# Diagonal tiles for the channels' own term, and a later store of the first batch's inputs, in a three-part decoder layer

## The chip, the core and the metric

One core of a Trainium2 chip runs the whole layer in one launch. The core has a matrix engine (TensorE, "PE" in the profile; its weight loads are "PEld"), a vector engine (VectorE, "DVE"), an activation engine (ScalarE, "ACT"), a general engine (GpSimd, "POOL") and a queue engine that mostly issues DMAs (SyncE, "SP"). ACT issues DMAs too. Each engine executes its own instructions strictly in the order in which they were laid down when the program was built, so an instruction that waits holds everything behind it on that engine, DMA issues included.

The metric is device time in microseconds (us) of one execution; lower is better.

## The reference, cut to what matters

Inputs are `x` (4 batches of 512 tokens by 512 channels), a context `ctx_1024` (4 by 512 by 256) and weights, all float32. Three sublayers follow one another, each with a residual sum and a layer norm:

1. Windowed attention: compress 512 channels to 256, make q, k and v, softmax attention with 16 heads in windows of 128 tokens with a relative bias, project back to 512.
2. A selective state-space layer (SSM). It takes the context as its input and the normed attention output as its gate `z`.
3. A gated feed-forward with quantized activations and ternary weights (512 to 2048 and back).

The change touches the second one. Its core, cut:

```
u     = silu(conv(in_proj_w @ ctx) + conv_b)          # 512 channels x 512 steps, per batch
x_dbl = x_proj_w @ u                                  # dt_lo (16 rows), Bm (16), Cm (16)
delta = softplus(dt_proj_w @ dt_lo + dt_proj_b)
state = state * exp(delta * A) + (delta * u) * Bm     # along time, 512 channels x 16 states
y     = sum over the 16 states of state * Cm
y     = y + D * u                                     # the channels' own part
out   = y * silu(z)
```

The last sum, `D * u`, is what the change calls the channels' own part of the outputs.

## The kernel before, in words

**Staging.** Every batch goes through three kinds of work: attention (threads `attn_c`, `attn_qk`, `attn_window`), the SSM (`ssm_inputs`, `ssm_steps`, `ssm_gate`) and the feed-forward (`ffn`, with `ffn_signs` turning the weights into signs once, by way of memory). Each of these is a Python generator. A weaver takes them in turn by times written out by hand (the constants `TP`, `T0`, `TA`, `TG`, `DT` and so on) and gives the instructions priorities from that. A planner then settles the order on each engine when the program is built, from these priorities, from data dependences, from free buffers and from its own model of how long each instruction takes. There is no run-time reordering between engines: what the planner laid down is what every queue does. So an edit at one place can alter the order elsewhere.

**The SSM's inputs (`ssm_inputs`).** Per batch, the projection and the convolution write `u`, a tile of 128 partitions by 4 channel groups (`e` = 0 to 3) by 512 steps. The whole `u` is stored to memory as `ud` (line 290, issued by ACT, 1 MB). Then PE makes `xd` from `u` (line 296), ACT copies it (line 297), and its B and C rows are stored as `bcd` (line 299, issued by ACT, 64 KB). `ssm_weights` loads these rows back, spread over partitions, as `bc` (line 347, issued by SP). PE makes `dt` (line 307), ACT the softplus into `sizes`. Line 319 then multiplies `sizes` by `u` **in place**, one instruction for each `e`: on DVE for the first batch, on POOL for the others. For the first batch's first channel group the product and `sizes` are spread over partitions by PE (line 328, tiles `du_ps` and `d_ps`) and copied out by DVE (line 332) and ACT (line 330). All other groups are stored as `dd` and `dud` (lines 335 and 336, SP) and loaded back spread out (line 367, SP).

**The SSM's steps (`ssm_steps`).** A batch has four channel groups `q` of 128 channels. A partition holds one of 32 channels with one of 4 states, so a group takes 4 channel blocks `j` (in two pairs `g`) times 4 state sets `n`. Per pair and `n`: POOL multiplies `du` by B (line 384), ACT makes `da` (line 388), DVE runs the recurrence (line 390), and DVE (line 392) or POOL (line 394) multiplies by C. PE then sums the 4 states of each channel into the output `y`, a PSUM bank of 128 channels by 512 steps. Block `j` goes to the 32 partitions from 32j on, as a matmul of 128 rows by 32 columns placed in column tile j (line 398, a float32 matmul is two instructions on PE). There is one `y` bank (`BY = 1`).

The group's own part opens that sum. `uq`, the group's slice of `ud`, is loaded by SP (line 355), and line 374 multiplies it by `own`, a 128 by 128 diagonal matrix of `D`:

```
with tc.issue_after(ssm_dt[0].ins) if b + q == 0 else ExitStack():
    nc.tensor.matmul(y, lhsT=own[:, q, :], rhs=uq, start=True, stop=False)
```

This happens 16 times (4 batches by 4 groups), 32 instructions on PE. For the first group of the first batch it is held behind the last spread matmul of line 328.

**Buffers.** The tag `yr` has two buffers of 128 by 512 (`BR = 2`). Before the change only `ssm_gate` uses them, to load finished outputs `y` back (line 425).

**DMA completion.** The issues of the SP and ACT queues take turns on eight completion counters, and an issue waits until the earlier transfer on its counter has landed.

## Time and profile before

| what | value |
|---|---|
| runs of before | 831.76, 842.35 and 834.16 us, median 834.16 us |
| the profiled execution | 833.79 us, its span on the core 832.0 us |
| mean granted TensorE clock | 0.951 of full speed |
| PE busy by stretch: 0 to 100 us | 82.9 of 100 us |
| PE busy, 100 to 500 us | 379.5 of 400 us |
| PE busy, 500 to 700 us | 170.0 of 200 us |
| PE busy, 700 us to the end | 121.6 of 132 us |
| first and last product of the SSM's steps (POOL, line 384) start at | 38.86 and 672.81 us |

How to read it: times in the profile are microseconds from the start of the span. A row of the timeline is start, duration, engine, line, operation, output<-inputs, shapes and count, and in square brackets how long the engine was idle before it and what ended the idle time. "SPq" and "ACTq" rows are DMA issues on those queues. "xN" is how many instructions a row merges; instructions on PE are pipelined and can overlap, so the time of a PE group is best taken from its start to the start of the next row. The chain of waits names, from the last instruction backwards, what released each step.

### The profile page before, as it was taken

The page shows a single profiled execution, that of the slowest core. Times are in us where ns is not written, and L with a number is a line of the kernel's source. Part 1 is how long each engine was busy: PE and PEld are TensorE (multiplying, and loading weights), DVE is VectorE, ACT ScalarE, POOL GpSimd, SP SyncE. Part 2 cuts the span into 40 slices and gives each one's busy share as a digit, 9 for nine tenths or more (in the row PEclk, how much of TensorE's full clock was granted, in tenths as well). Part 3 has the DMA queues.
Part 4 walks back from the last instruction along what each step waited for, and adds up shares of the span by engine and source line. Part 5 has one row for each costly group of instructions (what it writes and reads, how often), then busy time and mean ns, then how long its engine had stood idle before and what let it go on. Part 6 is the DMA issues. An engine that isn't in the chain of part 4 may idle for free.

```text
span 832.0 us, 11692 instructions
## 1 busy us (share of the span) xinstructions
PE 754.0 (91%) x3906; PEld 411.9 (50%) x3906; DVE 647.7 (78%) x943; ACT 591.2 (71%) x1037; POOL 557.4 (67%) x323
## 2 busy tenths in 40 slices
PE   9798899999899999899988998798887889999995
PEld 4233244444344444344434454365455657777773
DVE  5279586898999887989989799989999588453542
ACT  3568789787775976877797868696685847845651
POOL 2177489598678779787865968787889383333342
PEclk9797899999899999999999999999899999999998
DMA  7887688876243438564334384772251202301101
GB/s 216 300 275 222 225 263 306 307 220 211 91 140 103 149 83 264 190 230 143 107 108 126 106 288 170 216 275 97 94 162 37 70 8 102 95 20 51 52 26 51
DMA packets 82497, 128.97 MB, mean 155 GB/s; under 512 B 18659, under 2 KB 29043, under 8 KB 81157
## 3 DMA queue, kind: packets, MB, share of 16 engines
q1 hardware_dynamic: 65700, 108.51, 40.2%
q10 hardware_dynamic: 16736, 19.71, 6.9%
q8 instruction: 31, 0.51, 0.3%
q14 instruction: 30, 0.24, 0.1%
HBM read 91.22 MB, written 36.97 MB: 154 GB/s over the span
## 4 chain that ended last, share of the span: by engine, by line
PE 53%; DVE 20%; ACT 14%; DMA 5%; issue 5%; POOL 2%; SPq 1%; ACTq 0%; DVEq 0%; POOLq 0%
PE d_ps L824 9%; DVE da L390 6%; PE y L398 5%; PE sc_ps L628 5%; PE u_ps L796 4%; DVE state L390 4%; PE g_ps L772 3%; PE a_ps L695 3%; PE sc_ps L619 3%; ACT da L388 3%; PE c_ps L562 2%; PE sc_ps L656 2%; DVE state L392 2%; PE in_ps L273 2%; PE xd_ps L296 2%
## 5 line engine op out<-in xcount | busy, mean ns | idle before, releaser
L384 POOL TENSOR_TENSOR state<-du,bc 128x1024 f32<-128x1024 f32 x128 | 301.7, 2373 | 112.7 <-PE y L398 65.7
L388 ACT ACTIVATE da<-d,a_neg 128x512 f32<-128x512 f32 x256 | 174.9, 695 | 71.0 <-DVE state L392 37.7
L394 POOL TENSOR_TENSOR state<-state,bc 128x1024 f32<-128x1024 f32 x64 | 152.1, 2377 | 41.4 <-DVE state L390 27.5
L390 DVE TENSOR_TENSOR_SCAN state<-da,state 128x512 f32<-128x512 f32 x128 | 152.8, 1210 | 30.0 <-ACT da L388 21.6
L390 DVE TENSOR_TENSOR_SCAN da<-da,state 128x512 f32<-128x512 f32 x128 | 153.2, 1215 | 11.1 <-ACT da L388 11.1
L817 POOL TENSOR_TENSOR lo<-gs,hi 128x512 fp32r<-128x512 f32 x64 | 81.9, 1286 | 105.5 <-ACT hi L815 102.3
L398 PE MATMUL y<-state,sel 128*32 128x512 f32 x512 | 98.5, 649 | 6.4 <-DVE state L392 3.6
L392 DVE TENSOR_TENSOR state<-da,bc 128x512 f32<-128x512 f32 x128 | 84.9, 679 | 0.7
L652 ACT ACTIVATE sc<-sc_ps,ntop 128x128 f32<-128x128 f32 x256 | 74.0, 375 | 12.0 <-DVE ntop L636 10.9
L824 PE MATMUL d_ps<-sd,hi 128*128 128x512 f32 x256 | 74.5, 412 | 8.3 <-DVE gs L780 4.3
L772 PE MATMUL g_ps<-taken,sg 128*128 128x256 bf16 x512 | 69.4, 280 | 9.0 <-DVE x L867 4.3
L824 PE MATMUL d_ps<-sd,lo 128*128 128x512 f32 x256 | 75.7, 418 | 0.0
L628 PE MATMUL sc_ps<-k,q 32*128 32x256 f32 x256 | 73.6, 410 | 1.0 <-ACT q L584 1.0
L815 ACT CAST hi<-gs 128x512 fp32r<-128x512 f32 x64 | 38.8, 614 | 50.0 <-DVE gs L805 33.2
L796 PE MATMUL u_ps<-taken,su 128*128 128x256 bf16 x512 | 67.5, 273 | 6.7 <-DVE gs L805 5.5
L805 DVE TENSOR_TENSOR gs<-gs,u_ps 128x512 f32<-128x512 f32 x64 | 43.5, 682 | 38.3 <-PE u_ps L796 38.0
L780 DVE TENSOR_TENSOR gs<-g_ps,taken 128x512 f32<-128x512 f32 x64 | 43.4, 682 | 30.5 <-PE g_ps L772 30.5
L772 PEld LDWEIGHTS <-sg 128*128 128x128 fp8e4 x512 | 47.7, 100 | 33.7 <-issue 28.1
L796 PEld LDWEIGHTS <-su 128*128 128x128 fp8e4 x512 | 46.3, 98 | 29.0 <-issue 21.2
L628 PEld LDWEIGHTS sc_ps<-k,q 32*128 32x128 f32 x256 | 42.5, 187 | 30.1 <-issue 23.5
L824 PEld LDWEIGHTS d_ps<-sd,hi 128*128 128x128 f32 x256 | 45.0, 191 | 22.7 <-ACT hi L815 4.2
L636 DVE TENSOR_REDUCE ntop<-sc_ps 128x4 f32<-128x512 f32 x64 | 43.3, 679 | 15.1 <-PE sc_ps L628 15.0
(161 smaller groups left out, 1184.0 us busy)
## 6 DMA issues: line engine op xcount, KB each, us to landing
d<-dd SPq DMA_DIRECT2D x60, 256.0 KB, 4.3
du<-dud SPq DMA_DIRECT2D x60, 256.0 KB, 4.1
bc<-bcd SPq DMA_DIRECT2D x32, 256.0 KB, 4.3
xT<-in_xT_dram SPq DMA_DIRECT2D x16, 256.0 KB, 4.8
xa<-in_x_dram SPq DMA_DIRECT2D x16, 256.0 KB, 4.6
raw_sgd<-in_wgT_dram SPq DMA_DIRECT2D x16, 256.0 KB, 3.7
ud<-u ACTq DMA_DIRECT2D x4, 1024.0 KB, 8.2
uq<-ud SPq DMA_DIRECT2D x16, 256.0 KB, 2.7
```

The costliest lines, as they stand in the source:

```text
L384: nc.gpsimd.tensor_tensor(st, du, bb.unsqueeze(1).to_broadcast([P, 2, S]), ALU.mult)
L388: nc.scalar.activation(da, d[:, j, :], AF.Exp, scale=a_neg[:, a : a + 1])
L390: nc.vector.tensor_tensor_scan(to, da, st[:, j, :], 0.0, ALU.mult, ALU.add)
L392: nc.vector.tensor_tensor(st[:, j, :], da, cb, ALU.mult)
L394: nc.gpsimd.tensor_tensor(st, st, cb.unsqueeze(1).to_broadcast([P, 2, S]), ALU.mult)
L398: nc.tensor.matmul(y[ts(j, EB), :], lhsT=sel, rhs=sts[j], start=False, stop=(n == NG - 1), tile_position=(0, EB * j))
L628: nc.tensor.matmul(psc[:, ts(m, 2 * P)], lhsT=qT[rows_, m, tok], rhs=kT[rows_, m, :, tok], start=False, stop=(m == NM - 1), tile_position= ...
L652: nc.scalar.activation(sc[:, j, :], psc[:, ts(j, P)], AF.Exp, bias=ntop[:, h : h + 1])
L772: nc.tensor.matmul(pg[:, ts(j, HS)], lhsT=sg[:, c, ts(2 * f2 + j, P)], rhs=qT[:, c, :], start=(c == 0), stop=(c == NC - 1),)
L796: nc.tensor.matmul(pu[:, ts(j, HS)], lhsT=su[:, c, ts(2 * f2 + j, P)], rhs=qT[:, c, :], start=(c == 0), stop=(c == NC - 1),)
L817: nc.gpsimd.tensor_tensor(lo, g2, hi.bitcast(F32), ALU.subtract)
L824: nc.tensor.matmul(pos[t], lhsT=part[:, j, ts(t, P)], rhs=sd[:, 2 * f2 + j, :], start=(f2 + j == 0 and part is parts[0]), stop=(f2 == NF2 ...
```

## The change

Three edits, all in the SSM.

1. The own part is no longer one 128 by 128 matmul per group but four of 32 rows by 32 columns, the blocks on the diagonal of the same `own` tile, block `j` reading partitions 32j on of `uq`, writing partitions 32j on of `y`, and placed at row and column 32j of the array. Each opens its part of the sum.
2. For the first batch only, the store of `u` to `ud` is issued after the store of `bcd` and not before the `xd` matmuls.
3. For the first batch only, the products of `sizes` and `u` go to tiles of their own, named `due`, in the two buffers of tag `yr`, and not over `u`. The four products take these two buffers in turn.

```
-        nc.scalar.dma_start(out=ud, in_=u)
+        if b > 0:
+            nc.scalar.dma_start(out=ud, in_=u)
...
         nc.scalar.dma_start(out=bcd, in_=xd[DB:XD, :])
+        if b == 0:
+            nc.scalar.dma_start(out=ud, in_=u)
...
-            adder.tensor_tensor(u[:, e, :], ex, u[:, e, :], ALU.mult)
+
+            due = mp.tile([P, S], F32, tag="yr", name=f"due{e}", bufs=BR) if b == 0 else u[:, e, :]
+            adder.tensor_tensor(due, ex, u[:, e, :], ALU.mult)
...
-                    for k, src in (("du", u[:, e, :]), ("d", ex)):
+                    for k, src in (("du", due), ("d", ex)):
...
-            nc.sync.dma_start(out=dud[:, e, :], in_=u[:, e, :])
+            nc.sync.dma_start(out=dud[:, e, :], in_=due)
...
-                nc.tensor.matmul(y, lhsT=own[:, q, :], rhs=uq, start=True, stop=False)
+                for j in range(NQ):
+                    part = ts(j, EB)
+                    nc.tensor.matmul(
+                        y[part, :],
+                        lhsT=own[part, q, part],
+                        rhs=uq[part, :],
+                        start=True,
+                        stop=False,
+                        tile_position=(EB * j, EB * j),
+                    )
```

`NQ` is 4, `EB` is 32, and `ts(j, n)` is the slice from j times n to (j + 1) times n.

## The prediction

> **What bounds the kernel now.** I read the page's busy line first, then the chain of waits, then the order of time around the first product of the SSM, then PE's rows around line 374.

> ```profile
> PE 754.0 (91%) x3906; PEld 411.9 (50%) x3906; DVE 647.7 (78%) x943; ACT 591.2 (71%) x1037; POOL 557.4 (67%) x323
> ```

> No engine is full, but PE is near it: 379.5 of the 400 us from 100 to 500. The SSM's steps form the long thread, from 38.86 us to about 690; the list of waits shows POOL's products idle 65.7 us, in 27 stands, for line 398 to release state buffers, so PE's order sets that thread's pace. The feed-forward follows. Two things can therefore move the end: when the thread starts, and PE's time in it.

> The chain of waits at the start (start, length, what):

> ```profile
> 20.43 4.68 DMA xT<-in_xT_dram
> 25.18 8.23 DMA ud<-u
> 33.52 0.70 DVE u L319
> 34.27 3.78 PE du_ps L328 x4
> ```

> The store of `u` is on the path because line 319 overwrites `u`: it must wait until the store has read it. The same in order of time:

> ```profile
> 25.18 0.38 ACTq L290 DMA_DIRECT2D ud<-u  x1
> 25.61 0.68 ACT L297 ACTIVATE xd<-xd_ps,col 49x512 f32<-49x512 f32 x1 [2.99 <-DMA xT<-in_xT_dram]
> ...
> 26.96 0.35 ACTq L299 DMA_DIRECT2D bcd<-xd  x1
> ...
> 28.63 2.10 ACT L309 ACTIVATE sizes<-dt_ps 128x512 f32<-128x512 f32 x4
> ...
> 33.43 0.33 SPq L355 DMA_DIRECT2D uq<-ud  x1
> 33.52 2.50 DVE L319 TENSOR_TENSOR u<-sizes,u 128x512 f32<-128x512 f32 x4 [12.64 <-DMA ud<-u]
> 33.86 1.29 SPq L347 DMA_DIRECT2D bc<-bcd  x2
> ...
> 38.86 2.35 POOL L384 TENSOR_TENSOR state<-du,bc 128x1024 f32<-128x1024 f32 x1 [32.61 <-DVE du L332]
> ```

> Two stands end with the same landing. DVE was ready when the first softplus was (one takes 0.60 us, so 28.63 + 0.60 = 29.23) and starts at 33.52. SP issues nothing between 24.9 and 33.43, because its next instruction, `uq`, reads `ud`; the first `bc` loads stand behind it.

> **The products elsewhere: −4.2 us.** The in-place hazard goes. What is late next is the softplus, so line 319 starts near 29.28 instead of 33.52: 4.24 us. From there to the first POOL product took 5.34 us (one product, four `du_ps` passes, the copy), giving 34.6 instead of 38.86. If PE, with no idle time ahead of it, does its four passes in 1.9 us (row 40.68 us: 1.88 for four) and not 3.78, it is up to 1.9 us more.

> The tag `yr` has two buffers. The third product waits until the last `du_ps` pass has read the first `due` (its end was about 42.4, now about 38.2), and the fourth until the second one's `dud` store has landed (3.4 us median). Behind them on DVE stand copies of line 332 and the first scans. I cost this at nothing: DVE idles 2.96 us ahead of the copy at 41.74 and 3.15 ahead of the scan at 48.69, and the third group's first `dud` load is issued at 74 us, the fourth's later. Without that cover it is one landing, 3.4 us.

> **The store behind the projections: 0, bounds −0.7 and +1.7 us.** Both issues stay on ACT, in the other order; nothing is added. ACT issued `ud` at 25.18 after waiting for an earlier transfer's counter, and `bcd` at 26.96 for the next counter. Swapped, line 297 can begin when `xd_ps` ends (about 24.95) instead of 25.61, 0.66 us sooner, `bcd` goes at about 25.7, and `ud` at about 26.95 on the later counter, so the table load ahead of the softplus stays at 27.3. `bcd` (64 KB; stores of that size, the `sgd` ones, land in 3.5 us) is there by 29.2, `bc` (4.7 us) by 34.0: just ahead of the 34.6 above, if SP lets it go. The `ud` store now ends near 26.95 + 8.23 = 35.2, 1.8 us later, and `uq` with it. The first own pair ran at 45.83 and its first partner on line 398 at 53.65, so even moved 4 us forward it has `uq` (35.2 + 0.3 + 2.7 = 38.2) ahead of 41.5. If `uq` still stands ahead of `bc` or of the `dd` stores on SP, that queue stands until 35.2: +1.7.

> **The diagonal tiles: +1.5 us.** PE's rows, whose costs are from one start to the next:

> ```profile
> 100.05 1.07 PE L398 MATMUL y<-state,sel 128*32 128x512 f32 x8
> 101.04 0.50 PE L619 MATMUL sc_ps<-bias_hi,identr 128*128 128x512 f32 x1
> ...
> 131.32 1.02 PE L374 MATMUL y<-uq,own 128*128 128x512 f32 x2
> 132.27 0.43 PE L663 MATMUL a_ps<-scT,v 128*32 128x128 f32 x8
> ...
> 251.29 1.06 PE L398 MATMUL y<-state,sel 128*32 128x512 f32 x6
> 252.28 0.66 PE L656 MATMUL sc_ps<-ident,sc 128*128 128x128 f32 x4
> 252.87 1.04 PE L398 MATMUL y<-state,sel 128*32 128x512 f32 x2
> 253.85 0.33 PE L656 MATMUL sc_ps<-ident,sc 128*128 128x128 f32 x1
> ```

> Four column tiles take 0.99 us, three 0.99, one alone 0.98: tiles in different columns run side by side, and their number costs nothing. The own pair took 0.95 (two passes of 0.43 plus 0.09 where the array's shape changes). Eight diagonal instructions side by side take the 0.99 of the row x8. What is added is a change of shape on the side where there was none: at most 0.09 us for each of 16, 1.5 us in all. There is no gain in PE time to be had from this edit alone.

> No row shows tiles on different rows *and* columns. The bounds: one after another, eight passes of 0.43 are 3.43 us, 2.57 more than the 0.86 of now, 16 times, +41 us of PE. Below nothing: if they slip entirely under neighbouring tiles, 16 × 0.95 = −15 us. The nearest row, line 398, is the same bank, the same columns and the same form, so I take it. A second price: the planner may lay other matmuls between the four. Of line 398's 64 sums, 38 stand whole and the rest in pieces of 0.98 each; 0.44 extra pieces per sum would be 16 × 0.44 × 0.98 = 6.9 us. But those pieces come of states that are ready at different times, while the four own tiles wait for one load; I keep 6.9 for the range alone.

> [...]

> **The sum.** Against the profiled execution (832.0 us of span, 833.79 in all, 0.4 below the median of 834.16): 833.8 − 4.2 + 0 + 1.5 = 831.1, so **831 us**. The 4.2 should carry: the thread that starts earlier runs through stretches where PE always has work.

> **The rivals.**

> *The SP stand was the real brake: about 813 us.* For: SP sends everything late after 33.43, the first sign stores too; ACT then stands 3.91 us at 46.24 and 1.24 at 51.76 for sign stores, and 1.76 at 57.20, with the states' `da` behind it. If SP starts 4.9 us sooner (28.5) and these 6.9 us go too, that is 11.8; if the new order also spares the longest stand of POOL for line 398 (9.3 us), 21. Against: the DMA engines are busy 84% from 20 to 40 and 91% from 40 to 60, so earlier issues mostly queue.

> *The stand only moves: about 837 us.* `uq` stays ahead on SP, now until 35.2 (+1.7); the first `bc` lands after 39 and eats the 4.2; the fourth product's wait costs another part of its 3.4. 833.8 + 1.7 + 1.5 = 837. This is also the case in which the change doesn't do what it says.

> *The tiles do not run side by side: about 859 us, slower.* 11 of the 16 own pairs lie between 98 and 465 us, where PE is 95% full; 11 × 2.57 = 28 us, 831 + 28 = 859 (all sixteen: 872). It decides the sign at 2% once an own group costs over (850.8 − 831)/16 = 1.2 us more than now. An order in which PE makes the states wait for a split own group ends at the same place.

> **Chances.** Forecast 0.37, moved stand 0.15 (both within 2%, which is about what a measurement of this kernel can tell from no change: its runs span 831.76 to 842.35); SP as brake 0.26; tiles in a row or split on the path 0.22. The edits change the planner's order from 25 us on, and I cannot read that order from here; I hold the two outer cases this high because POOL's 65.7 us of stands for PE show how much lies in it. The forecast's own range, with −1.9 and +6.9 as its ends, is 829 to 838. For 8 times in 10 the range takes half of each outer case: 812 to 857. Faster by over 2% 0.25, within 0.53, slower 0.22.

> **What would show it.** Right: line 319 on DVE starts near 29.3 with no wait for `ud`; the first POOL product near 34.6; `bc` issued before `uq`; own instructions of 32 by 32 in groups of eight, about 1.0 us to the next row. Wrong: SP idle to 35; own instructions 0.43 us apart or in pieces; or the starts as predicted and the last line 398 no earlier than 687, in which case the order lost what the start gained.

## The result and the profile after

The changed kernel takes **874.25 us** (median; 871.40 to 878.20), the kernel before beside it 838.25 us (831.76 to 843.78). The ratio is **1.0451 [1.0394, 1.0508]**: slower by 4.5%, where 831 us was forecast and 857 was the upper end of the range. The profiled execution has a span of 876.4 us (878.20 in all), so 44.4 us are to be found against the 832.0 of before. (The medians lie 36 us apart: the profiled execution of after is the slowest of its four, and that of before, 833.79 us, is faster than the median.) Ratios here and below leave out executions that ran in a slower state, among them one of `b_diag` that took 1057.84 us at a mean clock of 0.637, while the medians in us are of all executions.

The page of the kernel after, with its first part and the granted clock of TensorE from its second (tenths of full speed in 40 slices; a 9 is 90% or more):

```profile
span 876.4 us, 11890 instructions
...
PE 795.4 (91%) x4002; PEld 424.1 (48%) x4002; DVE 654.9 (75%) x943; ACT 590.3 (67%) x1037; POOL 558.1 (64%) x323
...
PEclk9798969589989989898769998979999999999998
```

The same clock line of before:

```profile
PEclk9797899999899999999999999999899999999998
```

PE is busy for 41.4 us more with only 96 more instructions; the sums of DVE, ACT and POOL have moved by about 1% or less. The mean granted clock fell from 0.951 to 0.909. In the trace the clock is only ever full or half, and it was half for 160.9 us instead of 83.7. (Such times are taken here to the end of the execution, some 1.8 us behind the span's.)

**Where the 44.4 us lie.** The last product of the SSM's thread (line 384 before, 398 after) starts at 696.65 us instead of 672.81, which is 23.8 us. Behind it follow 179.8 us instead of 159.2, the other 20.6. These are two different losses.

*Ahead of the last product* the clock is at half for 153.6 us instead of 75.1. These 78.5 us more could cost up to 39 (an estimate: half of them), which is enough for the 23.8; whether they do is tested below. The same stretch by the windows view (stretch, length, busy us and count of PE, PEld, DVE, ACT and POOL, mean granted clock, DMA share, GB/s), of before:

```profile
100.00:200.00 100.00, 97.51 (x481) 45.20 (x480) 80.79 (x100) 82.92 (x172) 82.26 (x38) 0.95 0.81 271
```

and of after:

```profile
100.00:200.00 100.00, 94.09 (x386) 40.32 (x385) 69.92 (x83) 72.67 (x147) 66.95 (x31) 0.80 0.66 223
```

PE is busy nearly as long, but at a clock of 0.80 it gets through 386 matmuls instead of 481, and POOL through 31 instructions instead of 38. In the list of waits POOL's stands (times in which an engine stands idle and waits) for PE to release state buffers grow from 65.7 us to 81.8.

*Behind the last product* the clock is full in both kernels (0.98 and 0.99); there is more work left. PE is busy for 166.68 us from 697 to 876, and for 146.08 us from 673 to 832 before. PE's groups in those stretches (instructions, busy us, mean ns, idle before), of before:

```profile
L824 PE MATMUL d_ps<-sd,lo 128*128 128x512 f32 x164 | 47.1, 409 | 0.0
L824 PE MATMUL d_ps<-sd,hi 128*128 128x512 f32 x160 | 46.9, 413 | 1.5 <-ACT hi L815 0.9 <-DVE gs L780 0.6
L796 PE MATMUL u_ps<-taken,su 128*128 128x256 bf16 x312 | 41.1, 274 | 0.3 <-DVE gs L780 0.3
L772 PE MATMUL g_ps<-taken,sg 128*128 128x256 bf16 x256 | 33.4, 273 | 1.7 <-DVE gs L780 0.9 <-DVE x L867 0.7
```

and of after:

```profile
L838 PE MATMUL d_ps<-sd,lo 128*128 128x512 f32 x186 | 53.9, 409 | 0.0
L838 PE MATMUL d_ps<-sd,hi 128*128 128x512 f32 x184 | 53.6, 410 | 0.4 <-ACT hi L829 0.3
L810 PE MATMUL u_ps<-taken,su 128*128 128x256 bf16 x360 | 47.7, 274 | 0.7 <-DVE gs L819 0.7
L786 PE MATMUL g_ps<-taken,sg 128*128 128x256 bf16 x296 | 38.8, 273 | 1.7 <-DVE gs L794 0.9 <-DVE gs L819 0.8
```

Each matmul costs what it did, but 134 more of them (22 + 24 + 48 + 40) have been left for the end: work that before's order laid under the SSM.

**The start.** In order of time:

```profile
25.68 0.38 ACTq L302 DMA_DIRECT2D ud<-u  x1
...
26.82 0.35 ACTq L300 DMA_DIRECT2D bcd<-xd  x1
...
29.12 0.69 DVE L324 TENSOR_TENSOR due<-sizes,u 128x512 f32<-128x512 f32 x1 [7.62 <-ACT sizes L312]
...
33.07 0.33 SPq L360 DMA_DIRECT2D uq<-ud  x1
...
33.49 1.28 SPq L352 DMA_DIRECT2D bc<-bcd  x2
...
39.76 0.69 DVE L324 TENSOR_TENSOR due<-sizes,u 128x512 f32<-128x512 f32 x1 [8.59 <-ACT da L402]
40.38 0.68 DVE L337 COPY du<-du_ps 128x512 f32<-128x512 f32 x1
...
42.04 0.67 DVE L337 COPY du<-du_ps 128x512 f32<-128x512 f32 x1
...
42.80 2.34 POOL L398 TENSOR_TENSOR state<-du,bc 128x1024 f32<-128x1024 f32 x1 [36.37 <-DMA bc<-bcd]
```

The first product runs at 29.12, as forecast (29.3), but then DVE stands for 8.59 us ahead of the third one, with the copies of line 337 behind it. POOL begins at 42.80 instead of 38.86; its bracket names `bc`, but the second copy, which ends at 42.71, is what came just ahead of it. The store `ud` still goes ahead of `bcd`, and `uq` still ahead of `bc`.

**The tiles.** PE's rows around an own part that stayed whole, and around one that did not:

```profile
131.29 1.06 PE L381 MATMUL y<-uq,own 32*32 32x512 f32 x8
132.28 0.50 PE L707 MATMUL a_ps<-rows,one 2*128 2x512 f32 x1
...
409.78 1.74 PE L381 MATMUL y<-uq,own 32*32 32x512 f32 x2
411.45 3.78 PE L273 MATMUL in_ps<-hT,in_s 128*128 128x512 f32 x4
415.17 1.92 PE L381 MATMUL y<-uq,own 32*32 32x512 f32 x4
...
420.17 1.91 PE L381 MATMUL y<-uq,own 32*32 32x512 f32 x2
```

Eight instructions of four tiles take 0.99 us to the next row: they run side by side. At 409.78 the planner has laid other matmuls between the tiles of one group; the three pieces take 1.67 + 1.84 + 1.84 = 5.35 us at half clock.

So my reading was: neither the tiles' form nor the start is worth 44 us, and what is new is the order on every engine. The theories to be told apart were: **order** (the planner's new order makes the loss, whatever the tiles do), **form** (32 by 32 tiles cost PE time or clock), and **start** (the 4 us at the start grow on the way).

### The profile page after: what moved, and what is told of

It is laid out like the page before. It is cut to its first block, busy times and chain, and to the rows that moved or that the text cites. A ratio compares the mean times of both kernels' runs of the same rounds, so it can differ in the third digit from the quotient of the medians.

```text
span 876.4 us, 11890 instructions
## 1 busy us (share of the span) xinstructions
PE 795.4 (91%) x4002; PEld 424.1 (48%) x4002; DVE 654.9 (75%) x943; ACT 590.3 (67%) x1037; POOL 558.1 (64%) x323
## 3 DMA queue, kind: packets, MB, share of 16 engines
q1 hardware_dynamic: 65700, 108.51, 38.2%
## 4 chain that ended last, share of the span: by engine, by line
PE 43%; DVE 22%; ACT 10%; issue 7%; DMA 4%; POOL 3%; SPq 0%; ACTq 0%; DVEq 0%; POOLq 0%
PE d_ps L838 11%; DVE da L404 6%; DVE state L404 5%; PE y L412 5%; PE u_ps L810 5%; PE g_ps L786 4%; PE sc_ps L642 4%; PE sc_ps L633 2%; DVE state L406 2%; PE sc_ps L670 2%; ACT da L402 2%; PE y L381 2%; DMA acc<-x0d 2%; POOL state L398 2%; PE dt_ps L310 1%
## 5 line engine op out<-in xcount | busy, mean ns | idle before, releaser
L398 POOL TENSOR_TENSOR state<-du,bc 128x1024 f32<-128x1024 f32 x128 | 302.2, 2376 | 145.8 <-PE y L412 81.8
L402 ACT ACTIVATE da<-d,a_neg 128x512 f32<-128x512 f32 x256 | 177.0, 700 | 74.6 <-DVE state L406 40.2
L412 PE MATMUL y<-state,sel 128*32 128x512 f32 x512 | 101.3, 666 | 10.1 <-DVE state L406 9.7
L642 PE MATMUL sc_ps<-k,q 32*128 32x256 f32 x256 | 80.3, 438 | 0.0
L642 PEld LDWEIGHTS sc_ps<-k,q 32*128 32x128 f32 x256 | 46.3, 202 | 31.4 <-issue 25.2
L670 PE MATMUL sc_ps<-ident,sc 128*128 128x128 f32 x256 | 48.0, 321 | 9.3 <-ACT sc L666 9.1
```

The source lines that it names most:

```text
L398: nc.gpsimd.tensor_tensor(st, du, bb.unsqueeze(1).to_broadcast([P, 2, S]), ALU.mult)
L402: nc.scalar.activation(da, d[:, j, :], AF.Exp, scale=a_neg[:, a : a + 1])
L412: nc.tensor.matmul(y[ts(j, EB), :], lhsT=sel, rhs=sts[j], start=False, stop=(n == NG - 1), tile_position=(0, EB * j))
L642: nc.tensor.matmul(psc[:, ts(m, 2 * P)], lhsT=qT[rows_, m, tok], rhs=kT[rows_, m, :, tok], start=False, stop=(m == NM - 1), tile_position= ...
```

## The experiments

### Form and order, each without the other

`b_diag` takes before's order as it was laid down and replaces the own part's instructions where they stand; the first new one inherits the old one's waits, the last its releases. `a_full` does the opposite in the order of after.

```diff
+def swap_own(nc):                      # once the order is laid down; b_diag, on before
...
+        new = [
+            nc.tensor.matmul(
+                y[ts(j, EB), :],
+                lhsT=own[ts(j, EB), q, ts(j, EB)],
+                rhs=uq[ts(j, EB), :],
+                start=True,
+                stop=False,
+                tile_position=(EB * j, EB * j),
+            )
+            for j in range(NQ)
+        ]
...
+        # a_full, on after:
+        new = [nc.tensor.matmul(y[:, :], lhsT=own[:, q, :], rhs=uq[:, :], start=True, stop=False)]
```

> Every engine keeps the order of the kernel before, instruction for instruction; alone the 16 own pairs are replaced where they stand by the four diagonal tiles each (no other edit). Theory O (the planner's new order costs the time): no slower than before by over 1%, 834 to 842 us, since 16 changes of shape are worth 1.5 us. Theory T (the diagonal tiles themselves cost it, by running one after another or by letting the matrix engine's clock drop): 855 us or more, with more of the span at half clock than the 84 us of before.

> Every engine keeps the order of the changed kernel; alone the own parts are put back to one 128 by 128 matmul each, where the first of the four tiles stood. The products' own tiles and the later store stay. Theory O: as slow as the changed kernel, 866 to 878 us. Theory T: back to 834 to 845 us. If both have a share, it is read from the two runs together: this one less before is the order with the other two edits, the changed kernel less this one is the form of the tiles.

| order | own part whole | own part as four tiles |
|---|---|---|
| before's | 1 | b_diag: 834.74 us, 0.9969 [0.9935, 1.0004] |
| after's | a_full: 864.74 us, 1.0342 [1.0293, 1.0391] | after: 874.25 us, 1.0451 [1.0394, 1.0508] |

The four tiles cost nothing that can be told in before's order. After's order with the whole matmul back in it is 3.4% slower (it still has the other two edits, see below). So most of the loss is the order's. The form adds about 1% within it by these two rows, but that share is not firm: `own_alone` below has nearly the same order and the split tiles without the other two edits, and cannot be told from `a_full`.

The trace of `b_diag` shown here comes from one more execution of the same program:

> The same program as the run with before's order and diagonal tiles, looked at once more for a profile at the usual clock (the first one was taken in an execution of 1057.84 us at a mean clock of 0.637). Theory O: 16 groups of eight own instructions, each about 0.99 us to the next row at full clock, time at half clock near before's 84 us, span 828 to 842 us. Theory T: over 110 us at half clock.

It took 832.54 us beside 832.49 for before; its span is 830.8 us, the clock 0.953, the last product starts at 671.6 us, with 159.1 us behind it. The own part's instructions, by its tile view (ns least/median/most, first and last start):

```profile
L946 PE MATMUL y<-uq,own x128: 587/600/612, 45.3 to 662.9; 32*32 32x512 f32 x128
```

Of the 16 groups, 14 take 0.991 us to the next row. **Form is out, for an order in which the four stand together.**

### One edit at a time, each with its own order

`own_alone` has the first edit only (four matmuls in place of one, and the planner lays down what it will); `due_alone` only the products in buffers of their own.

> Only the diagonal tiles, planned as a whole; products in place, store as before. The order it is given is the changed kernel's to over 99% on PE, DVE and SP and wholly on ACT and POOL. Theory O and theory T: 866 to 878 us, as the changed kernel. A value in the middle would say that the start's stall (the products) had a large share after all.

> Only the products' own tiles; the own part is one matmul and the store of u stands where it stood. The order on ACT and POOL is that of before, PE, DVE and SP keep 99% of theirs. In the changed kernel DVE stood 8.6 us ahead of the third product, which was laid ahead of the copies of the spread products, so the first POOL product started at 42.8 us and not at 38.9. Theory: this alone does the same, first product at 42 to 43 us, and the span grows by at most those 4 us: 834 to 842 us. The prediction's step (first product at 34.6 us) would give 830.

`own_alone`: 868.86 us, 1.0369 [1.0300, 1.0439]. Its last product starts at 691.0 us with 179.8 us behind it: the whole loss, nearly, from this edit. Its order parts from before's after PE's first 42 matmuls. By the longest sequence that two orders have in common, 83% of PE's instructions stand as in before's order, 62% of DVE's and 65% of ACT's (the expectations below count more narrowly and give lower shares). Against after, 99% is the same.

`due_alone`: 840.98 us, 1.0017 [0.9967, 1.0068]. Its order is before's, but for 1%. At the start, its DVE rows:

```profile
29.43 1.29 DVE L321 TENSOR_TENSOR due<-sizes,u 128x512 f32<-128x512 f32 x2 [9.17 <-ACT sizes L309]
39.97 0.69 DVE L321 TENSOR_TENSOR due<-sizes,u 128x512 f32<-128x512 f32 x1 [9.24 <-DMA dud<-due]
40.58 0.68 DVE L334 COPY du<-du_ps 128x512 f32<-128x512 f32 x1
```

Two products run early; the third takes a buffer of `yr` whose content is still being stored to `dud`, and waits 9.24 us for that landing (in after, where the bracket of the same stand names an ACT instruction that ended at that moment, it is 8.59). The first POOL product comes at 43.01, 4.15 us later than before, and the end is not measurably later.

The second edit alone, the store moved behind the projections, was not run: with it the planner lays down the same order on every engine as without it.

### Is any new order that bad?

If before's order is one good draw among many, an edit that adds next to no work must cost too, as soon as it makes the planner lay down something else. Four kernels change one of the hand-written constants by a little; three add no instruction, and `null_warm` adds one warming matmul at the start, some 0.9 us:

```diff
-TP = (-45, 50, 100, 170)
+TP = (-45, 51, 100, 170)     # null_tp
-AQ = 18
+AQ = 17                      # null_aq
-WARM = 3
+WARM = 4                     # null_warm
-AW = 10
+AW = 10.2                    # null_aw
```

> The kernel before with one hand-written time moved by one unit (the second batch's inputs due at 51, not 50). No instruction is added or taken away; the planner then gives PE 63%, DVE 45%, ACT 43% of the old order. Theory O1 (the order before is a chosen one, and nearly any other costs some per cent): 848 to 875 us. Theory O2 (something in the four tiles makes the changed kernel's order bad, other orders do not): 830 to 846 us. In both the span should stand at 790 to 800 us plus half of the time that the matrix engine's clock is at half, as in the five traces so far.

> The kernel before with the start of the attention's q and k moved by one unit (17 ahead of a batch's first window, not 18). No work added; PE keeps 62%, DVE 36%, ACT 34% of the order. O1: 848 to 875 us. O2: 830 to 846 us.

> The kernel before with a fourth warming matmul at the start (one pair more on PE at 5 us, 0.9 us). PE keeps 84%, DVE 54%, ACT 36% of the order. O1: 848 to 875 us. O2: 830 to 846 us.

> The kernel before with the distance between attention windows at 10.2 units, not 10. No work added; PE keeps 79%, DVE 60%, ACT 54% of the order, the nearest of the four to before. O1: 840 to 875 us. O2: 830 to 846 us.

| kernel | us, ratio [95%] | PE's order kept | half clock, us | last product starts | behind it |
|---|---|---|---|---|---|
| before | 836.78 beside the next four, 838.75 beside `own_alone` | | 83.7 | 672.8 | 159.2 |
| null_tp | 903.23, 1.0769 [1.0694, 1.0844] | 80% | 165.3 | 758.5 | 144.7 |
| null_aq | 861.33, 1.0279 [1.0215, 1.0344] | 81% | 93.9 | 680.6 | 176.4 |
| null_warm | 859.17, 1.0253 [1.0195, 1.0312] | 84% | 114.3 | 703.4 | 156.3 |
| null_aw | 849.23, 1.0169 [1.0080, 1.0258] | 85% | 90.4 | 678.7 | 164.0 |
| own_alone | 868.86, 1.0369 [1.0300, 1.0439] | 83% | 150.7 | 691.0 | 179.8 |

All four are slower, by 1.7 to 7.7%, and `null_tp` lies above the 848 to 875 us that were expected for it. The loss lies now ahead of the last product, now behind it, now in both. Nor does the clock explain all of it. The expectation's sum was 790 to 800 us plus half of the time at half clock; the span less that half is 798 us for `null_aw`, but 803 for `null_warm`, 810 for `null_aq` and 820 for `null_tp`, whose last product comes 85.7 us later with only 81.6 us more at half clock. A start time moved from 50 to 51 costs more than the change studied here. Each of the five edits that moved the order made the kernel slower, while `due_alone` left the order as it was and cost nothing that can be told. So a loss of this size comes with a new order whatever the edit is, and nothing here makes it a price of diagonal tiles.

### Is the clock a cause, or only a mark of waiting?

A slow clock could be the effect of PE standing about. To test it, PE was given more to do: in `a_full`'s order, matmuls that add zeros (an off-diagonal block of the identity, which is zero, times an input) to the open output bank were laid ahead of PE instructions that wait over 0.7 us, 37 pairs of them (the fillers); nothing else moved. `b_fill` has 32 such pairs in before's order.

```diff
+            for a, b in ((0, 64), (64, 0)):
+                nc.tensor.matmul(
+                    y[0][b : b + 64, :],
+                    lhsT=ident[a : a + 64, b : b + 64],
+                    rhs=in_s[a : a + 64, 0, :],
+                    start=False,
+                    stop=False,
+                    tile_position=(a, b),
+                )
```

> The run with the changed kernel's order and whole own matmuls, with 37 fillers laid in front of PE instructions that its trace shows waiting over 0.7 us (a filler is a pair of 64 by 64 blocks of zeros, side by side, added to the open output bank: all rows of the array work, the sums do not change, some 0.95 us each). PE gets more work, every other engine keeps its order. Theory K (the half clock that follows PE's stands is what costs the time): time at half clock falls from 129 us to under 95, and the kernel from 864.7 to 840 to 852 us. Theory S (the stands themselves cost it, the clock only goes along): 860 to 875 us whatever the clock does.

> The kernel before with its own order and 32 such fillers in front of the PE instructions that its trace shows waiting over 0.7 us. Theory K: time at half clock falls from 84 us to under 60, and the kernel from 837 to 818 to 828 us, under both kernels. Theory S: 836 to 850 us.

`a_fill`: 848.80 us, 1.0127 [1.0078, 1.0175], against 1.0342 without fillers. The granted clock of `a_full`, slice by slice:

```profile
PEclk9798999589989999899889988879998999999998
```

and with the fillers:

```profile
PEclk9899999999999899999998899989998999999998
```

The time at half clock falls from 129.3 us to 54.1, the last product starts at 667.2 us instead of 682.3. Adding some 35 us of work to PE (37 pairs of about 0.95) brought the SSM's thread forward by 15 us, past before's 672.8. POOL's stands for PE fall from 81.1 us to 66.7, near before's 65.7. So **the clock is a cause** in `a_full`'s order; for the 14 us by which the last product of after itself comes later than `a_full`'s (696.65 against 682.3) it was not tested. Behind the last product 179.8 us follow, as in `a_full` (179.3): the fillers do not touch that part, and it is what still parts `a_fill` from before. `b_fill`: 833.99 us, 0.9965 [0.9921, 1.0010]; half clock 66.8 us instead of 83.7, and no gain that can be told. The expectation by the clock, under 60 us at half clock and 818 to 828 us in all, was missed on both counts.

How the clock is lost can be seen in one place. PE's rows in the kernel after:

```profile
155.09 1.06 PE L412 MATMUL y<-state,sel 128*32 128x512 f32 x8 [2.61 <-DVE state L406]
157.78 0.66 PE L677 MATMUL a_ps<-scT,v 128*32 128x128 f32 x8 [1.62 <-ACT scT L672]
158.37 0.80 PE L633 MATMUL sc_ps<-bias_hi,identr 128*128 128x512 f32 x1
...
159.52 2.07 PE L642 MATMUL sc_ps<-k,q 32*128 32x256 f32 x4
```

In `a_full` the same two stood longer:

```profile
152.69 1.07 PE L412 MATMUL y<-state,sel 128*32 128x512 f32 x8 [3.14 <-DVE state L406]
155.38 0.66 PE L677 MATMUL a_ps<-scT,v 128*32 128x128 f32 x8 [1.63 <-ACT scT L672]
```

And `a_fill`, which is `a_full` with fillers in front of the two that wait:

```profile
149.93 1.06 PE L412 MATMUL y<-state,sel 128*32 128x512 f32 x8 [0.42 <-DVE state L406]
150.93 1.07 PE L1012 MATMUL y<-in_s,ident 64*64 64x512 f32 x4
152.62 0.43 PE L677 MATMUL a_ps<-scT,v 128*32 128x128 f32 x8 [0.62 <-ACT scT L672]
152.98 0.50 PE L633 MATMUL sc_ps<-bias_hi,identr 128*128 128x512 f32 x1
...
153.64 1.12 PE L642 MATMUL sc_ps<-k,q 32*128 32x256 f32 x4
```

Behind two stands of 2.61 and 1.62 us close together the clock is at half, in after from 157.4 to 181.3 us and in `a_full` from 153.7 to 177.6: the scores of line 642 then take 2.07 us for four instead of 1.12. They have 32 rows, and in after the clock stays at half while PE works through them and other matmuls, busy for 23.52 of these 23.89 us. With the stands filled, it is full from 43.8 to 275.9 us.

### The start, with the missing buffers

`due_four` is `due_alone` with a place for each of the four products:

```diff
-            due = mp.tile([P, S], F32, tag="yr", name=f"due{e}", bufs=BR) if b == 0 else u[:, e, :]
+            home = (("yr", BR), ("yr", BR), ("yq", 1), ("part", BP))[e]
+            due = mp.tile([P, S], F32, tag=home[0], name=f"due{e}", bufs=home[1]) if b == 0 else u[:, e, :]
```

> The kernel before with the first batch's products in four tiles of their own that nobody else holds then (two of tag yr, one of yq, one of part), so that neither the store of u nor the second product's store holds DVE. The order is before's to over 99%. If the prediction's start were right but for the two buffers, the first POOL product starts at 34.6 us; if the B rows are late next (their load stands behind uq on SP until 33.4), at 38 to 39. The end: if a start's microseconds carry to the end, 4 us under before at 34.6 and 0 at 38.5; due_alone, 4 us later at the start, ended level, so I expect 830 to 840 us either way.

837.06 us, 0.9987 [0.9948, 1.0026]. At its start:

```profile
28.59 2.52 DVE L322 TENSOR_TENSOR due<-sizes,u 128x512 f32<-128x512 f32 x4 [7.38 <-ACT sizes L309]
...
33.37 0.33 SPq L358 DMA_DIRECT2D uq<-ud  x1
...
33.79 1.28 SPq L350 DMA_DIRECT2D bc<-bcd  x2
...
37.49 4.64 POOL L387 TENSOR_TENSOR state<-du,bc 128x1024 f32<-128x1024 f32 x2 [31.29 <-DMA bc<-bcd]
```

All four products run without a stop, as the prediction had it for the change itself, and what is late next is `bc`: SP still stands for `uq` until 33.37. Of the 4.24 us, 1.37 arrive at POOL (37.49 for 38.86), and none that can be measured at the end. What `bc` ahead of `uq` on SP would give was not run.

## Why the prediction was wrong

**The step that failed is the order.** The prediction ended its sum with the edits' own costs and wrote: "The edits change the planner's order from 25 us on, and I cannot read that order from here". It gave that a chance, not a price, and let the sum stand on rows of an order that was no longer there. By the runs, the new order costs 3.4% with the whole matmul in it (`a_full`), and the costs of the edits in before's order are all within 0.3% (`b_diag` 0.9969, `due_alone` 1.0017, `due_four` 0.9987; the store never moved). In the changed kernel's trace the 44.4 us are 23.8 ahead of the SSM's last product and 20.6 behind it, where 134 feed-forward matmuls are left over. What was missing can be had from before's kernel alone: four edits that add next to no work cost 1.7 to 7.7%. A term for "another order", with that spread, was the largest of the sum.

**The diagonal tiles, +1.5 us: right in before's order.** The 0.99 us taken from line 398's rows is what eight instructions took, and `b_diag` shows no loss: four tiles in four row groups shared one bank in 0.99 us, not in the 3.43 of eight passes one after another.

**"The planner may lay other matmuls between the four", 6.9 us: right that it happens.** I kept it for the range alone, since "the four own tiles wait for one load". They were split all the same, at 409.78 and again at 595 us, and after's median is 9.5 us above `a_full`'s (874.25 against 864.74). The two splits make three extra pieces, 2.9 us at the 0.97 us that one takes at full clock (595.42 us of after, to the next row; an estimate). In the traces, `a_full`'s 129.3 us at half clock became 160.9, which may be the rest; that was not tested.

**The products elsewhere, −4.2 us: wrong twice.** The start of line 319's work was right (29.12 for 29.3). "I cost this at nothing" was wrong of the third product's wait. I had that one wait for PE's passes and only the fourth for a store; it was the third that waited for the store. The two buffers were not taken in turn: the planner gave the second, third and fourth product the same one, since PE reads the first product from the other until its last spread pass (from 43.8 us on). I took the cover from DVE's idle time *after* it, but the copies of line 332, which POOL waits for, stand behind it on DVE. The uncovered wait was not one landing of 3.4 us either, but 8.59 (9.24 in `due_alone`), because the store must first be issued by SP, behind `uq` and the first `bc` loads. So the first POOL product came at 42.80, not 34.6. And "the 4.2 should carry" was wrong of both signs: 4.15 us lost at the start (`due_alone`) and 1.37 gained (`due_four`) were both gone at the end.

**The store behind the projections, 0: right by luck.** The sum had the two issues swapped at no cost; they were never swapped. The planner issues `ud` first all the same, so the edit does not do what it says, as the rival *The stand only moves* had it.

**The rivals.** *The stand only moves* described the start well (`bc` behind `uq`, a later first product), and its 837 us is what `due_alone` and `due_four` give; it is not what the change gave. *Tiles not side by side*, 859 us, named the right side with the wrong mechanism. Its last sentence, on an order in which PE makes the states wait, comes nearest: POOL's stands for PE did grow by 16 us; but the cause is not a split own group, since `a_full` has none and has 81.1 us of them. *The SP stand as the brake* was not tested, as SP's stand stayed in every run.

**PE's clock** was in none of these. The prediction read "No engine is full, but PE is near it" from the busy share and priced added PE time; it did not ask at which clock that share was worked off, nor what stands of 1 to 3 us do to it.

What stays open: by which of its costs the planner lays a different order for four tiles than for one matmul; why this order leaves 134 feed-forward matmuls to the end; and whether an order exists in which the change gains. None of the kernels run is faster than before by a margin that can be told.

## What to carry to other kernels

Where a planner lays down the order, the price of an edit that moves the order is its own cost plus that of a new draw: run one or two edits that add no work first, to see how wide that draw is, and where it is wide, test an edit in the old order before judging it. Read PE's busy share together with its granted clock: an engine 94% busy at a clock of 0.80 is far from full, and work added to its stands can win time (`a_fill` against `a_full`, 848.80 against 864.74 us). When an in-place product gets a buffer of its own, count the buffers against the products, and ask who stands behind the first that must wait.

## What the hardware showed

| clock in the piece | share with 128 rows | pieces | in the next one |
|---|---|---|---|
| full | 0.5 and more | 379 | 0 fall to half |
| full | 0.4 to 0.5 | 12 | 2 fall |
| full | 0.3 to 0.4 | 21 | 19 fall |
| full | under 0.3 | 14 | 14 fall |
| half | under 0.8 | 31 | 0 rise |
| half | 0.8 to 0.9 | 6 | 4 rise |
| half | 0.9 and more | 32 | 29 rise |

In 15 pieces at half clock PE was busy for more than 95% of the time, but with 128 rows for less than 80%; the rest was mostly matmuls of 32 rows (the scores, 29% of the time of all 15) and 17 (`dt`, 24%), and the clock was at half in the next piece all 15 times. These are counts of two traces; what sets the clock they do not show.

**Diagonal tiles share a bank.** Four float32 matmuls of 32 by 32, in four row groups and four column groups, ran side by side into one PSUM bank in 0.99 us (131.29 us of after), as fast as four column tiles of 128 rows (0.99 at 100.05 us of before).
